# A linear-attention stack: the first half group in front, its causal mask by a product and ScalarE, carried sums by ScalarE, fp4 weights later, spreads from sixteen rows

## Chip, cores and metric

One NeuronCore of a Trainium2 chip. The metric is the device time of one launch in microseconds (us). A TensorE matmul is called a product of TensorE; VectorE is DVE, ScalarE is ACT, GpSimd is POOL and SyncE is SP in the profile.

## The reference

Input x is 8 sequences of 1024 rows of 256 numbers, all float32. Four residual blocks follow each other, each fed with a layer norm of x:

```python
x = x + L0_attn(_layernorm(x))   # linear "flow" attention, 16 heads of 16, with its own FFN (gelu)
x = x + L0_ffn(_layernorm(x))    # 256 -> 1024 relu -> 256
x = x + L1_attn(_layernorm(x))   # softmax attention over 1024 rows, one head of 256
x = x + L1_ffn(_layernorm(x))    # fp4-quantised gate/up (704) and down
```

The linear attention is causal. With q and k the sigmoids of projections, it needs running sums over the rows (cumsum) of k and q, from which per row and head the flows `sink_in` and `src_out` come; then running sums of k and q weighted by these flows; from them a weight for each source row and a scale for each target row; and last the causal product of q with the running sum of k times v:

```python
sink_in = normal / einsum(q + EPS, cumsum(k) + EPS)
src_out = normal / einsum(k + EPS, cumsum(q) + EPS)
cons_sink = einsum(q + EPS, cumsum(k * src_out) + EPS) / normal
cons_src  = clip(einsum(k + EPS, cumsum(q * sink_in) + EPS) / normal, -1, 1)
src_comp = exp(cons_src) / cumsum(exp(cons_src)) * normal
x = einsum(q * sink_in / normal, cumsum(k x (v * src_comp))) * sigmoid(cons_sink)
```

## The kernel before

**Tiling.** Rows go in chunks of 128; a group p is four chunks (512 rows), so there are 16 groups, two to a sequence. The linear attention of a group is `linear_group` (L863). `front` (L873) normalises and transposes a chunk. `linear_span` (L919) works on a span of chunks: the projections and sigmoids (`k`, `q`, [head dimension on partitions, rows along the free axis]); `running` (L806), which is a scan of VectorE along the rows (`prod`); a fused product with the other of q and k (EPS added); `head_sums` (L748), small products with `hsum` that add the 16 dimensions of each head; the reciprocal `r1` and `flow`; the spreading of `flow` from one row per head back to 16 rows; the same with weighted q and k (`weighted`); and from these `e`, `div` and `scale`, and again a spreading, by which q is multiplied. Each of these waits for the one before. Sums that run over a span's end are carried by a copy of the scan's last column (`carry_cur`, `carry_w`). Group 0 alone is cut into two spans of two chunks ("near"); its spreading is done by TensorE with mask tiles (`spread_near`, L785). All other groups spread through memory (`spread`, L763): `flow` is written to a flat DRAM tile, and each of the tiles is read from there with each head's row repeated 16 times.

**Chunks.** `linear_chunk` (L1079) makes v, `qz` (q masked to the even or odd heads by two ScalarE operations), the scores in four PSUM banks of 128x512, their causal mask (`sc`, a product with an upper triangle), the values, the carried sum `kv`, the output product with Wo, a layer norm (`u`, `h`), and the transposes that feed the FFN's half tiles.

**Filling.** `dense` (L1269) is the two FFNs of a group, in halves of 256 rows, 8 steps of 4 products each (`half,w_ff`, then `w_ff,hidden`); a step reads 256 KB of weights through five buffers `w_ff`, whose loads are `load_weights` (L1314). `norms_1`, `norms_2`, `soft_chunk` (softmax attention and the fp4 FFN for a chunk), `fp4_weights` (L645; 18 pieces quantised on VectorE, loaded as `w_raw`, worked with `q_c`) and `softmax_weights` are further parts.

**Order.** All parts are generators. `Plan` (L63) records every instruction in the order in which it takes parts, and this order is pinned on each engine: an engine never passes a waiting instruction. `Plan.took` (L157) holds estimated costs of each operation, a ring time for DMA among them, and `Plan.run` (L267) takes the part that can start first by these estimates, then the riper, then the one with the lower due time `at`. All DMAs are issued by SP, in that order.

Of the kernel before, what the change touches and what calls it, by code (L numbers as in the profile page):

```python
# [9 lines left out]
F32 = mybir.dt.float32  # L10
# [52 lines left out]
class Plan:  # L63
# [12 lines left out]
    def __init__(self, tc, nc):  # L76
# [15 lines left out]
        self.tiled = False  # L92
        self.parts = []
# [63 lines left out]
    def took(self, queue, op, args, kw):  # L157
# [12 lines left out]
        if queue == "tensor":  # L170
# [5 lines left out]
            if tiled:  # L176
                cost *= 0.25
# [24 lines left out]
        for ap in aps:  # L202
            name = ap.tensor.name
            if self.by.get(name) != queue:
                start = max(start, self.done.get(name, 0.0))
            if name not in self.done and name in self.held:
                start = max(start, self.used[name])
        end = start + cost
        if queue == "sync":
            n = 4e-6 / 160e-3  # L210
# [56 lines left out]
    def run(self):  # L267
        while self.parts:
            now = self.free.get("tensor", 0.0)
            best = None  # L270
            for part in self.parts:
# [5 lines left out]
                wait = max(max(t) - now - (0.3 if stays else 0.0), 0.0)  # L277
                unripe = max(t[1] + self.RIPE[queue] - now, 0.0)
# [48 lines left out]
def block_stack_kernel(ctx: ExitStack, tc: tile.TileContext, a: dict, out: bass.AP):  # L327
# [115 lines left out]
    pos = const.tile([P, P], F32, name="pos")  # L443
    nc.vector.tensor_copy(pos, pos_i)
# [20 lines left out]
    mask_tiles = [make("prob", "mask") for _ in range(2)]  # L465
    late = set()

    def masks():
        yield act(ident, at=0.02)
        for b in range(4):  # L470
# [12 lines left out]
    def late_constants():  # L483
# [10 lines left out]
        late.add("hsum")  # L494
        yield dve()
# [3 lines left out]
        for g in range(NG):  # L499
            yield dve()  # L500
            nc.vector.tensor_scalar(rpos[:, g, :], pos, float(g * GT), None, ALU.add)
            yield dve()
            nc.vector.reciprocal(rpos[:, g, :], rpos[:, g, :])
# [141 lines left out]
    def fp4_weights():  # L645
# [15 lines left out]
        for i, (src, turns) in enumerate(pieces):  # L661
            for j in range(i, min(i + 3, len(pieces))):
                if j not in raws:
# [3 lines left out]
                        dma(at=0.9 + 2.2 * i / len(pieces), when=lambda: count["stage"] == 4),  # L667
# [7 lines left out]
            at = 0.9 + 2.2 * i / len(pieces)  # L675
# [87 lines left out]
    def spread(packed, tiles):  # L763


        width = packed.shape[0] // 32 * P
        flat = hbm.tile([32, GT], F32, tag="packed", name="packed", bufs=4)
        yield dma(packed)
        nc.sync.dma_start(
            out=flat[:, :width].rearrange("r (t l) -> t r l", l=P), in_=packed  # L770
        )
        out = {}
        for b in tiles:
            t = out[b] = yield from fresh("flow", dma(flat), "spread")
            nc.sync.dma_start(
                out=t[:, :width],
                in_=bass.AP(
                    tensor=flat.tensor,
                    offset=flat.offset + 8 * b * GT,
                    ap=[[GT, 8], [0, DH], [1, width]],  # L780
# [25 lines left out]
    def running(out, cur, carry, b, first, last):  # L806
# [9 lines left out]
        if not last:  # L816
            nc.vector.tensor_copy(carry[:, b : b + 1], out[:, cur.shape[1] - 1 :])
# [45 lines left out]
    def linear_group(p):  # L863
# [34 lines left out]
        for i in range(G):  # L898
            plan.start(front(i), p + 0.03 * i)
# [19 lines left out]
    def linear_span(p, span, fronts, tiles):  # L919
# [13 lines left out]
        after = 0.25 if span.start else 0.0  # L933
        near = len(span) < G

# [32 lines left out]
        for n, b in enumerate((2, 0, 3, 1)):  # L968
            other = (b + 2) % 4
            prods[other] = yield from fresh(  # L970
                "flow", dve(cur[b], at=p + 0.15 + 0.04 * n + after, when=turn("flow")), "prod"
            )
            prod = prods[other][:, :width]
            running(prod, cur[b], past["cur"], b, opens, closes)
            yield dve(cur[other])
            nc.vector.scalar_tensor_tensor(prod, cur[other], ATT_EPS, prod, ALU.add, ALU.mult)
# [6 lines left out]
        nc.vector.scalar_tensor_tensor(flow, pos[rows], float(g * GT), r1, ALU.add, ALU.mult)  # L983
# [7 lines left out]
        for n, b in enumerate((2, 0, 3, 1)):  # L991
            other = (b + 2) % 4
            w = weighted[b]
            need = dve(w, at=p + 0.35 + 0.04 * n + after, when=turn("scale"))
            if near:
                weighted[b] = yield from fresh("flow", need, "weighted")
            else:
                yield need
            out = weighted[b][:, :width]
            nc.vector.tensor_tensor(out, cur[b], w[:, :width], ALU.mult)  # L1000
            if near and n % 2:
# [620 lines left out]
```

## Time and profile before

| | |
|---|---|
| median of three runs | 2690.91 us (2689.86 to 2692.45) |
| the profiled execution | 2683.94 us |
| its span | 2682.2 us |
| mean granted TensorE clock | 0.991 |
| ACT_TABLE_LOAD | 308, 395.2 us |
| DMA | 209.92 MB, mean 78 GB/s |
| `w_ff` loads | 1024 issues of 128 KB |
| `spread` reads | 90 issues of 256 KB |
| `packed` writes | 30 issues of 64 KB |

A row of instructions gives engine, operation, output and input tile; all of the kernel's own have one line, that of the recorder (L308), so tiles tell them apart. An f32 matmul is recorded as two instructions. In a table of stretches each engine has its busy time and count, then follow the granted TensorE clock (1.00 is full), the share of the 16 DMA engines' time and GB/s.

### The profile page before, as it was taken

The numbers are of one execution on the slowest core, as the hardware profiler recorded it, in microseconds if no ns is written. First come the engines' busy times: TensorE is split into PE (matmuls) and PEld (weight loads), VectorE is DVE, ScalarE is ACT, GpSimd is POOL, SyncE is SP. The second block draws the span as 40 slices with busy tenths as digits, with TensorE's granted clock in tenths as the row PEclk, the third lists the DMA queues.
The fourth block names the chain that finished last, engine by engine and source line by source line (L and its number), as shares of the span: only waits on it lengthen the run. The fifth ranks groups of instructions, "written<-read, shape, count | busy, mean of one in ns | idle before, by whom it ended". The sixth has DMA issues, their size and how long they took to land.

```text
span 2682.2 us, 45602 instructions
## 1 busy us (share of the span) xinstructions
PE 2597.4 (97%) x16687; PEld 2014.0 (75%) x16687; DVE 1969.3 (73%) x4514; ACT 1246.7 (46%) x2430; POOL 560.5 (21%) x1101
## 2 busy tenths in 40 slices
PE   6999999999999999999999999999999999999997
PEld 4777777777777777777777777777777777787765
DVE  8889687776858668686776858778586776856576
ACT  2443445535455453645536354363635536344343
POOL 1232232221212213122131212212121131212000
PEclk8999999999999999999999999999999999999999
DMA  3334222312223222232322223132231322322100
GB/s 87 107 105 143 89 82 64 108 59 89 73 69 106 66 86 73 69 96 71 91 73 76 80 75 106 52 92 75 70 108 54 98 63 71 89 66 81 41 12 12
DMA packets 282135, 209.92 MB, mean 78 GB/s; under 512 B 23864, under 2 KB 270392, under 8 KB 281912
## 3 DMA queue, kind: packets, MB, share of 16 engines
q1 hardware_dynamic: 281912, 207.00, 25.9%
q8 instruction: 133, 2.18, 0.3%
q14 instruction: 90, 0.74, 0.1%
HBM read 188.17 MB, written 18.74 MB: 77 GB/s over the span
## 4 chain that ended last, share of the span: by engine, by line
PE 80%; DVE 12%; DMA 2%; issue 1%; ACT 1%; POOL 1%; SPq 0%; DVEq 0%; ACTq 0%
PE bank L308 80%; DVE hid L308 2%; DVE prod L308 1%; DVE n L308 1%; DVE ln_st L308 1%; DMA spread<-packed 1%; DVE x_amax L308 1%; DVE u L308 1%; DMA w_ff<-in_L_attn_W_dram 1%; DVE res L308 1%; POOL ln_rstd L308 1%; DVE div L308 1%; DVE e L308 0%; DVE q L308 0%; DVE ln_mv L308 0%
## 5 line engine op out<-in xcount | busy, mean ns | idle before, releaser
L308 PE MATMUL bank<-half,w_ff 128*128 128x256 f32 x2048 | 533.6, 383 | 14.5 <-DMA w_ff<-in_L_ffn_w_dram 6.0
L308 PE MATMUL bank<-w_ff,hidden 128*128 128x256 f32 x2048 | 530.4, 383 | 7.7 <-issue 6.6
L308 PEld LDWEIGHTS bank<-half,w_ff 128*128 128x128 f32 x2048 | 379.4, 191 | 91.4 <-issue 26.6
L308 PEld LDWEIGHTS bank<-w_ff,hidden 128*128 128x128 f32 x2048 | 371.1, 191 | 96.0 <-issue 50.7
L308 ACT ACT_TABLE_LOAD x308 | 395.2, 1283 | 75.2 <-PE bank L308 71.1
L308 POOL TENSOR_SCALAR ln_ve<-ln_mv 128x1 f32<-128x1 f32 x384 | 96.0, 250 | 1320.7 <-DVE ln_mv L308 1299.4
L308 ACT ACTIVATE hidden<-bank,c_L_ffn_b 128x256 f32<-128x256 f32 x256 | 121.1, 473 | 338.0 <-PE bank L308 336.7
L308 PE MATMUL bank<-n2T,qT 128*128 128x512 f32 x512 | 241.4, 594 | 0.9 <-ACT qT L308 0.9
L308 POOL TENSOR_TENSOR ln_rstd<-ln_ve,neghalf 128x1 f32<-128x1 f32 x384 | 229.4, 597 | 32.0
L308 PE MATMUL bank<-vt,probT 128*128 128x256 f32 x1024 | 232.2, 380 | 0.0
L308 PEld LDWEIGHTS bank<-vt,probT 128*128 128x128 f32 x1024 | 193.2, 190 | 30.3 <-issue 3.3
L308 ACT ACTIVATE hidden<-bank,c_L_attn_b 128x256 f32<-128x256 f32 x256 | 121.4, 474 | 177.0 <-PE bank L308 175.4
L308 PE MATMUL bank<-wdT,hqT 128*128 128x256 f32 x768 | 178.0, 382 | 1.8 <-ACT hqT L308 1.8
L308 PE MATMUL bank<-wgT,xqT 128*128 128x352 f32 x512 | 173.4, 461 | 1.1 <-ACT xqT L308 0.9
L308 PE MATMUL bank<-wuT,xqT 128*128 128x352 f32 x512 | 172.4, 459 | 0.0
L308 DVE TENSOR_TENSOR sc<-bank,triu 128x512 f32<-128x512 f32 x256 | 159.4, 679 | 5.3 <-PE bank L308 3.8
L308 PEld LDWEIGHTS bank<-wdT,hqT 128*128 128x128 f32 x768 | 145.4, 191 | 22.8 <-ACT hqT L308 2.8
L308 DVE TENSOR_TENSOR hid<-hid,bank 128x352 f32<-128x352 f32 x118 | 60.9, 516 | 133.8 <-PE bank L308 92.0
L308 POOL TENSOR_TENSOR xr<-xr,b_L_attn_ln_b 128x256 f32<-128x256 f32 x64 | 49.3, 788 | 482.6 <-DMA xr<-in_L_attn_inputs_dram 482.6
L308 PEld LDWEIGHTS bank<-n2T,qT 128*128 128x128 f32 x512 | 93.6, 190 | 69.5 <-issue 62.7
L308 PEld LDWEIGHTS bank<-wuT,xqT 128*128 128x128 f32 x512 | 97.3, 190 | 54.2
L308 PEld LDWEIGHTS bank<-wgT,xqT 128*128 128x128 f32 x512 | 92.6, 190 | 37.0 <-issue 3.8
(214 smaller groups left out, 4384.4 us busy)
## 6 DMA issues: line engine op xcount, KB each, us to landing
w_ff<-in_L_attn_W_dram SPq DMA_DIRECT2D x512, 128.0 KB
w_ff<-in_L_ffn_w_dram SPq DMA_DIRECT2D x512, 128.0 KB
spread<-packed SPq DMA_DIRECT2D x90, 256.0 KB
x<-in_L_attn_inputs_dram SPq DMA_DIRECT2D x64, 128.0 KB
xr<-in_L_attn_inputs_dram SPq DMA_DIRECT2D x64, 128.0 KB
rows<-res SPq DMA_DIRECT2D x64, 128.0 KB
out_dram<-y SPq DMA_DIRECT2D x64, 128.0 KB
rows<-rows SPq DMA_DIRECT2D x56, 128.0 KB
```

The lines of the kernel that those rows point to most:

```text
L308: ins = method(*args, **kw)
```

## The change

Seven edits go together.

1. The parts of group 0's first span (chunks 0 and 1) get due times below zero. `Plan.run` calls these urgent: it does not hold them back until they are ripe, and lets them start up to 0.3 us late in front of others.
2. The recorder's estimates: a bf16 product costs a quarter, a product within 2.1 us after 2 us of TensorE's rest costs double, and a DMA's ring time goes by 250 GB/s in place of 160.
3. In group 0 the causal mask is no longer a VectorE product. A bf16 tile `later` (in a `q_c` buffer until group 0's last chunk) holds -2^100 above the diagonal and, in its last 128 columns, the identity; a product of these is put into each score bank first, the scores are added to it, and ScalarE's ReLU copies the bank to `sc`.
4. The carried columns are copied by ScalarE, and scans come in pairs: scan, scan, fused product, fused product.
5. The fp4 weights' due times run from 1.5 to 3.1 in place of 0.9 to 3.1.
6. `spread` writes the flat tile twice, side by side, and reads 16 source rows, each repeated 8 times, in place of 8, each repeated 16 times.
7. `pos` holds the positions of both groups of a sequence, so that `flow`, `e` and `rpos` need fewer operations, and the two products of `kv` with the block diagonal become one.

```diff
@@ Plan.took
-            if tiled:
+            if tiled or op == "matmul" and kw["lhsT"].dtype == BF16:
                 cost *= 0.25
...
+        if queue == "tensor":
+            if start - self.ran > 2.0:
+                self.slow = start + 2.1
+            if start < self.slow:
+                cost *= 2
+            self.ran = start + cost
         end = start + cost
         if queue == "sync":
-            n = 4e-6 / 160e-3
+            n = 4e-6 / 250e-3
@@ Plan.run
-                wait = max(max(t) - now - (0.3 if stays else 0.0), 0.0)
-                unripe = max(t[1] + self.RIPE[queue] - now, 0.0)
+                wait = max(max(t) - now - (0.3 if stays or part[2] < 0.0 else 0.0), 0.0)
+                urgent = part[2] < 0.0
+                unripe = 0.0 if urgent else max(t[1] + self.RIPE[queue] - now, 0.0)
@@ constants
-    pos = const.tile([P, P], F32, name="pos")
-    nc.vector.tensor_copy(pos, pos_i)
+    pos = const.tile([P, NG, P], F32, name="pos")
+    for g in range(NG):
+        nc.vector.tensor_scalar(pos[:, g, :], pos_i, float(g * GT), None, ALU.add)
...
+    later = make("q_c", "later")[:, : GT + P]
...
+        nc.scalar.copy(later[:, GT:], ident)
...
+        nc.vector.tensor_scalar(
+            later[:, :GT].rearrange("p (n t) -> p n t", n=4),
+            triu.unsqueeze(1).to_broadcast([P, 4, P]),
+            -1.0, 2.0**100, ALU.add, ALU.mult,
+        )
@@ fp4_weights
-                        dma(at=0.9 + 2.2 * i / len(pieces), when=lambda: count["stage"] == 4),
+                        dma(at=1.5 + 1.6 * i / len(pieces), when=lambda: count["stage"] == 4),
...
-            at = 0.9 + 2.2 * i / len(pieces)
+            at = 1.5 + 1.6 * i / len(pieces)
@@ spread
-        flat = hbm.tile([32, GT], F32, tag="packed", name="packed", bufs=4)
+        flat = hbm.tile([32, 2, GT], F32, tag="packed", name="packed", bufs=4)
         yield dma(packed)
-        nc.sync.dma_start(
-            out=flat[:, :width].rearrange("r (t l) -> t r l", l=P), in_=packed
-        )
+        for e in range(2):
+            nc.sync.dma_start(out=flat[:, e, :].rearrange("r (t l) -> t r l", l=P), in_=packed)
...
-                    offset=flat.offset + 8 * b * GT,
-                    ap=[[GT, 8], [0, DH], [1, width]],
+                    offset=flat.offset + 8 * b * 2 * GT,
+                    ap=[[GT, 16], [0, DH // 2], [1, GT]],
@@ running
         if not last:
-            nc.vector.tensor_copy(carry[:, b : b + 1], out[:, cur.shape[1] - 1 :])
+            yield act(out)
+            nc.scalar.copy(carry[:, b : b + 1], out[:, cur.shape[1] - 1 :])
@@ linear_group
-            plan.start(front(i), p + 0.03 * i)
+            plan.start(front(i), p + 0.03 * i - (p == 0 and i < 2))
@@ linear_span
-        after = 0.25 if span.start else 0.0
+        after = 0.25 if span.start else -1.0 if near else 0.0
...
-        for n, b in enumerate((2, 0, 3, 1)):
-            other = (b + 2) % 4
-            prods[other] = yield from fresh(
-                "flow", dve(cur[b], at=p + 0.15 + 0.04 * n + after, when=turn("flow")), "prod"
-            )
-            prod = prods[other][:, :width]
-            running(prod, cur[b], past["cur"], b, opens, closes)
-            yield dve(cur[other])
-            nc.vector.scalar_tensor_tensor(prod, cur[other], ATT_EPS, prod, ALU.add, ALU.mult)
+        for n, pair in enumerate(((2, 0), (3, 1))):
+            for b in pair:
+                need = dve(cur[b], at=p + 0.15 + 0.08 * n + after, when=turn("flow"))
+                prod = prods[(b + 2) % 4] = (yield from fresh("flow", need, "prod"))[:, :width]
+                yield from running(prod, cur[b], past["cur"], b, opens, closes)
+            for b in pair:
+                yield dve(cur[b], prods[b])
+                nc.vector.scalar_tensor_tensor(
+                    prods[b], cur[b], ATT_EPS, prods[b], ALU.add, ALU.mult
+                )
...
-        nc.vector.scalar_tensor_tensor(flow, pos[rows], float(g * GT), r1, ALU.add, ALU.mult)
+        nc.vector.tensor_tensor(flow, pos[rows, g, :], r1, ALU.mult)
...
-        nc.vector.scalar_tensor_tensor(e, pos[rows], float(g * GT), e, ALU.add, ALU.mult)
-        nc.vector.tensor_scalar(e, e, src[rows], None, ALU.mult)
+        nc.vector.scalar_tensor_tensor(e, e, src[rows], pos[rows, g, :], ALU.mult, ALU.mult)
@@ linear_chunk
+        at = p - (p == 0 and i < 2)
...
+        by_act = p == 0
...
+        banks = [mm_bank() for _ in range(4)]
+        for bank in banks:
+            if by_act:
+                nc.tensor.matmul(
+                    bank, lhsT=later[:, GT:], rhs=later[:, :GT], start=True, stop=False,
+                    skip_group_check=True,
+                )
...
-                    start=True,
+                    start=not by_act,
...
+            if by_act:
+                nc.scalar.activation(sc, bank.rearrange("p (n t) -> p n t", n=4), AF.Relu)
+                scores.append(sc)
+                continue
...
-            for k in range(2):
-                nc.vector.tensor_tensor(
-                    new[:, k, :].rearrange("p (r d) -> p r d", r=4),
-                    kvbank[:, k, :].unsqueeze(1).to_broadcast([P, 4, 32]),
-                    bdiag.rearrange("p (r d) -> p r d", r=4),
-                    ALU.mult,
-                )
+            nc.vector.tensor_tensor(
+                new.rearrange("p k (r d) -> p k r d", r=4),
+                kvbank.unsqueeze(2).to_broadcast([P, 2, 4, 32]),
+                bdiag.rearrange("p (r d) -> p r d", r=4).unsqueeze(1).to_broadcast([P, 2, 4, 32]),
+                ALU.mult,
+            )
```

## The prediction

> **What bounds the kernel now.** I read the page first (busy shares), then the stretches, then TensorE's waits, then the timeline. The page's first part:
>
> ```profile
> PE 2597.4 (97%) x16687; PEld 2014.0 (75%) x16687; DVE 1969.3 (73%) x4514; ACT 1246.7 (46%) x2430; POOL 560.5 (21%) x1101
> ```
>
> TensorE is the bound: of 2682.2 us only 84.8 are idle. So a change can win in three ways only: less TensorE work, less idle, or less work done at half clock. The stretches say where the idle is (after the stretch and its length: busy time of PE, PEld, DVE, ACT, POOL; clock; DMA share; GB/s):
>
> ```profile
> 0.00:72.30 72.30, 46.75 (x334) 33.78 (x335) 58.35 (x157) 19.40 (x47) 14.27 (x37) 0.80 0.32 81
> 72.30:128.90 56.60, 56.59 (x423) 44.50 (x421) 46.94 (x115) 28.85 (x67) 17.44 (x35) 0.99 0.36 106
> 128.90:150.00 21.10, 14.49 (x91) 11.82 (x91) 20.13 (x38) 5.51 (x16) 8.83 (x12) 0.84 0.57 152
> 200.00:250.00 50.00, 43.90 (x248) 35.53 (x247) 44.64 (x104) 18.93 (x43) 11.92 (x23) 0.93 0.46 138
> 2600.00:2682.20 82.20, 67.76 (x290) 48.55 (x288) 53.77 (x118) 27.49 (x53) 2.95 (x8) 0.97 0.04 13
> ```
>
> 25.6 us idle lie before the first FFN matmul at 72.3, 6.6 in 128.9 to 150, 6.1 in 200 to 250, 14.4 at the end; the 2160 us from 340 to 2500 hold 22.7, 1%. Shorter stretches show the half clock of the front:
>
> ```profile
> 36.00:40.00 4.00, 2.99 (x16) 2.83 (x15) 3.67 (x8) 0.63 (x3) 0.00 (x0) 0.50 0.00 0
> 40.00:44.00 4.00, 4.00 (x15) 2.94 (x15) 2.70 (x8) 0.21 (x1) 0.00 (x0) 0.50 0.00 0
> 44.00:48.00 4.00, 4.00 (x18) 2.89 (x21) 2.81 (x8) 1.70 (x4) 0.00 (x0) 0.50 0.00 0
> 68.00:72.00 4.00, 4.00 (x15) 3.36 (x15) 2.12 (x6) 1.10 (x3) 0.26 (x2) 0.50 0.01 2
> ```
>
> After the idle of 25 to 30 us the clock is 0.50 to about 49, and again from 64 to 73. What TensorE waits for in the first 72.3 us, and later for weights (total us, times, longest):
>
> ```profile
> PE bank L308 <- DVE prod L308: 9.1, 6, 4.3
> PE bank L308 <- DVE scale L308: 3.4, 1, 3.4
> ...
> PE bank L308 <- DMA w_ff<-in_L_ffn_w_dram: 6.0, 2, 5.7
> PE bank L308 <- DMA w_ff<-in_L_attn_W_dram: 5.9, 3, 4.3
> ```
>
> It waits for VectorE's serial chain. Its marks in the timeline (start, length):
>
> ```profile
> 23.10 0.42 DVE L308 TENSOR_TENSOR weighted<-k,bank 128x256 f32<-128x256 f32 x1 [1.73 <-PE bank L308]
> 35.30 0.28 DVE L308 TENSOR_TENSOR e<-bank,rpos 64x128 f32<-64x128 f32 x1
> 40.08 0.28 DVE L308 TENSOR_TENSOR scale<-e,div 64x128 f32<-64x128 f32 x1
> 50.19 4.87 DVE L308 TENSOR_TENSOR sc<-bank,triu 128x512 f32<-128x512 f32 x8
> 65.44 0.29 DVE L308 TENSOR_TENSOR scale<-e,div 64x128 f32<-64x128 f32 x1
> 72.34 1.63 PE L308 MATMUL bank<-half,w_ff 128*128 128x256 f32 x4
> ```
>
> **The front, first span put first.** In the old order VectorE interleaves span 0 (chunks 0, 1) with span 1 (chunks 2, 3); in the new one span 1's scans stand behind. I add old durations in the new order. The first normalised tile goes ahead of the hsum copies and two rpos additions, but a mask operand of 128x512 (0.55, from 0.31 for 128x256) comes in: the first hsum matmuls end at about 19.6 (was 20.05). One group of projections instead of two stands before the first spreading matmuls (1.0 less): `weighted` at 22.0. From there to `e`: 4 products 0.42, 4 scans 0.70, 4 fused products 0.43, two span-1 scans 0.74, waits for ScalarE 0.5: 8.2, so `e` at about 30 (was 35.3). To `scale`: 0.3 + 0.34 + ScalarE 0.6 + matmul and copy 0.6, with two products and a scan of span 1 queued ahead of `div`, then 0.48 + 0.28 + 0.94 + 0.3 + 0.34 + 0.28 (one operation of 0.28 less): about 35 (was 40.1). Transpose, spreading (2.07 at half clock), two q products: q is scaled at 38.2, ScalarE's qz is out at 39.9 (was 46 to 47.8). TensorE is later than that: v projections, 4.1 at half clock, end at 41.6.
>
> **The mask.** Per chunk of group 0: four bf16 matmuls of 128x512 before the scores, then four ReLU copies on ScalarE for four VectorE products of 0.68. No bf16 matmul is in the trace. The nearest row is one recorded instruction of 512 f32 columns (n2T,qT: x4 in 1.88, 0.43 apart); an f32 matmul takes two of them (0.86), the upper end; the lower end is 0.11, a 128-column transpose. I take 0.43, doubled at half clock. Chunk 0's masks end at 45.0. "TensorE: Matmul & The Clock Gate", section "Wait — 56ns, not 53.3ns?", gives 215.7 ns for 512 columns when warm; by it all sixteen would cost 3.5, and the sum would be some 5 us lower. ReLU: the nearest row is ACT prob 128x512, 0.68, the same as VectorE's. From 37.4 to 72.3 ScalarE is busy 6.0 of 34.9 us, VectorE 27.2, so the work goes to the idler engine: 16 x 0.68 = 10.9 us leave it. Queued behind the eight ReLUs on ScalarE are the copies of k and xo (0.37 each), which TensorE awaits.
>
> From 45.0: scores 1.2 to 2, eight ReLUs to 51 to 52, value matmuls, kv by POOL 0.79, second chunk's xo, wo, then u 0.42, statistics 0.6, POOL 0.75, 0.47, h 0.77: chunk 1's h at about 62.5, the first FFN matmul at 63.4 (was 72.3): **-8.9**. Not done by then and done before: one hsum 0.46, total 0.3, transpose 0.2, two v projections 1.72, spreading 1.03: **+3.7**. The first FFN pair ran at half clock before (1.63 against 0.86): **-0.8**. Masks of chunks 2 and 3: 8 x 0.43 = **+3.4**. Span 1's `scale` is now later: VectorE has about 11 us queued ahead of it from 60.7 and ScalarE has Exp between two table loads (1.28 each), so near 75.6 where it was 65.4. What covers it is the first half's FFN, 8 x 1.72 = 13.8, and the wqk products, 4; what sticks out I put at **+2**, from 0 to 5.
>
> The clock page (same title, "What's actually happening") has the array warm after about 3.4 us of sustained work. The rows differ: 40 to 48 are fully busy and still at 0.50. By the page the new front would be warm from 39 and some 3 us shorter; I go by the rows.
>
> **Carried sums by ScalarE.** 72 VectorE copies of 0.15 (0.25 to 0.3 with the gaps before and after) become ScalarE copies of 0.15. New wait: the fused product overwrites the sum that ScalarE reads, so VectorE stands until the copy is through; behind it are the other products of its queue and, for TensorE, the hsum matmuls. Scans go in pairs, so one wait per pair, 0.3, up to 1.3 behind a table load: 4 pairs in each of 8 opening groups, from -0.5 to +1.3 each. Past 340 us VectorE is 73% busy and TensorE 99%: **0**. Without that cover it would be up to 42. The merged kv product (112 x 0.28 to 56 at about 0.48), the merged e and flow: VectorE alone, **0**.
>
> **Fp4 weights later, spreads.** The 18 pieces keep their DMAs and about 3 us of VectorE each; they only leave 73 to 150, where VectorE is at 83 to 95%. TensorE's waits for n and w_raw from 140 to 340 are 3.4; fewer pieces ahead of n on VectorE take about half: **-1.5** (0 to -3.4). Each spread's flat copy is written twice: 30 more SP issues of 0.57, 64 KB each, ahead of weight loads on SP; SP's issues are not what ends TensorE's waits, so 0 to +1 in each group, taken 0. The reads of 256 KB (x90) take 16 source rows in place of 8. The 5.7 wait at 129 comes with four such reads in flight:
>
> ```profile
> 128.90:135.00 6.10, 0.38 (x3) 0.20 (x3) 5.89 (x10) 0.33 (x2) 0.65 (x1) 0.72 0.92 224
> ```
>
> Share 0.92 at 224 GB/s: nearly all engines already work, so 1 MB takes some 4.7 us whatever its split. "DMA: Bandwidth & Descriptors", section "Why a DMA increments its semaphore by 16 and not by 1", holds that a DMA goes over as many engines as divide its outermost dimension, so 8 before. By it the four reads shrink by about 4 us and the two long waits nearly go, some 10 off; the share speaks for less. The two waits (5.7, 4.3) and their half-clock restarts (1.3, 1.5) are 12.8: from 0 to -12.8, and as weights still queue behind the spread I take half: **-6.4**.
>
> **Sum.** The end (14.4 idle) is the last chunk's chain, which no edit touches; a new order may move it by some us either way: 0. -8.9 + 3.7 - 0.8 + 3.4 + 2 - 1.5 - 6.4 = -8.5. The profiled execution took 2683.94 (span 2682.2, 1.7 around it), so 2675.4; the median of the runs, 2690.91, is 7.0 above it, so 2682.4.
>
> **Rivals.** *A, both gains in full.* FFN starts near 58 (mask matmuls at the low end, no waits in span 1) and both weight waits go: -13 + 3.7 + 1 - 13 = -21, 2670. For it: 25.6 idle in front. Against: the chain of VectorE stays serial.
> *B, given back.* FFN starts earlier, but span 1, now behind, leaves TensorE without work at the second half, and weights are as late as before: -8.5 + 6.4 + 3 = about +1, 2692. For it: VectorE was 81% busy in the front.
> *C, slower.* The recorder takes the rings at 250 GB/s instead of 160, and so orders FFN matmuls ahead of weights that have not landed. Pure FFN takes 256 KB in 1.72 us (152 GB/s) beside the spreads, and the trace's best in 4 us is 244. Its place is the weight wait in each of the 15 later groups; at 1.3 us each, 20 - 8.5 = +11, 2702. It decides from (8.5 + 5.4) / 15 = 0.93 each. Against: after 340 those waits were 1.9 in total.
>
> **Numbers.** A measurement of this kernel tells 0.2%, 5.4 us, from no change. Forecast (2676 to 2688) 0.42, A 0.22, B 0.22, C 0.14. Faster takes A and nine tenths of the forecast (the rest is above 2685.5), 0.6; same gets B's larger part, 0.23; slower C and what is left of B, 0.17. The range 2666 to 2698 leaves out A's far end and most of C.
>
> **What would show it.** Right: the first FFN matmul near 63; `e` and `scale` of span 0 near 30 and 35; no `sc` by VectorE before 150; the wait for w_ff in 125 to 150 under 3 us; idle from 340 on within 5 us of before. Wrong: a long wait of TensorE for span 1's `scale` or ScalarE's `sc` after 63, or w_ff waits in every group.

## The result: a little slower, and the profile after

The changed kernel takes 2694.57 us (median of 12 runs, 2686.36 to 2699.39), the kernel before, run beside it, 2691.81 (12 runs, 2685.18 to 2696.22): a ratio of 1.0012, 95% interval [1.0003, 1.002]. The forecast was 2682.4 and "faster". The profiled execution after took 2695.86 us (span 2694.2), 1.3 above its median; the one of before lies about 8 below its own, so the two profiles differ by 12 us where the medians differ by 2.8. Of a difference between the two profiles some 9 us are such chance.

The page's first part, after:

```profile
PE 2607.3 (97%) x16701; PEld 2021.4 (75%) x16703; DVE 1942.7 (72%) x4353; ACT 1261.6 (47%) x2521; POOL 587.6 (22%) x1101
```

VectorE is relieved as the change says (1969.3 to 1942.7 us), ScalarE takes some of it, TensorE has 9.9 us more busy time, and its idle time (span less busy) is 86.9, from 84.8.

The stretches of the front and of the weight waits, after (stretch, length, busy time of PE, PEld, DVE, ACT, POOL, clock, DMA share, GB/s):

```profile
0.00:72.30 72.30, 50.45 (x356) 37.19 (x358) 48.01 (x129) 30.56 (x77) 15.04 (x39) 0.81 0.30 84
72.30:128.90 56.60, 52.90 (x400) 39.89 (x400) 45.80 (x113) 27.87 (x73) 17.34 (x32) 0.97 0.32 93
128.90:150.00 21.10, 17.25 (x101) 13.97 (x100) 18.90 (x38) 5.99 (x14) 6.48 (x11) 0.92 0.63 172
200.00:250.00 50.00, 44.11 (x245) 34.40 (x243) 38.45 (x82) 19.79 (x51) 11.34 (x21) 0.97 0.47 137
```

Up to 72.3 TensorE is busy 3.7 us longer than before, from 72.3 to 128.9 it is busy 3.7 us less, from 128.9 to 150 2.8 more. The front's gain in busy time is given back in the next stretch, and 2.7 us of the 3.7 lie near 100: TensorE waits 1.84 for `n` and 0.85 for `h`.

The marks of the front in the timeline, after (start, length):

```profile
27.97 0.42 DVE L316 SCALAR_TENSOR_TENSOR prod<-k,prod 128x256 f32<-128x256 f32 x1 [2.11 <-ACT carry_w L316]
...
34.62 0.28 DVE L316 TENSOR_TENSOR e<-bank,rpos 64x128 f32<-64x128 f32 x1 [0.93 <-PE bank L316]
...
38.86 0.28 DVE L316 TENSOR_TENSOR scale<-e,div 64x128 f32<-64x128 f32 x1
...
76.54 0.29 DVE L316 TENSOR_TENSOR scale<-e,div 64x128 f32<-64x128 f32 x1
```

```profile
62.97 1.59 PE L316 MATMUL bank<-half,w_ff 128*128 128x256 f32 x4 [0.46 <-ACT half L316]
```

The first FFN product starts at 62.97 (before 72.34, forecast 63.4); span 0's `e` and `scale` are at 34.62 and 38.86 (before 35.30 and 40.08), not at 30 and 35. The first line shows one reason: VectorE waits 2.11 us for ScalarE's copy of one column (`carry_w`, at 27.75), which is queued behind a ScalarE operation that itself waits for TensorE. The other is the clock. The stretches of 14 to 28 us, after and then before:

```profile
14.00:18.00 4.00, 1.46 (x10) 0.55 (x8) 2.84 (x7) 1.59 (x8) 2.32 (x3) 1.00 0.16 41
20.00:24.00 4.00, 4.00 (x15) 3.16 (x15) 1.23 (x3) 0.47 (x1) 0.00 (x0) 0.50 0.85 236
24.00:28.00 4.00, 4.00 (x14) 3.24 (x13) 1.82 (x5) 0.75 (x3) 0.00 (x0) 0.50 0.53 130
```

```profile
14.00:18.00 4.00, 2.46 (x15) 1.47 (x13) 3.65 (x10) 1.68 (x5) 1.27 (x2) 1.00 0.65 191
20.00:24.00 4.00, 4.00 (x27) 3.39 (x26) 2.10 (x4) 0.95 (x2) 0.00 (x0) 1.00 0.60 158
24.00:28.00 4.00, 1.43 (x8) 0.74 (x8) 3.69 (x11) 1.96 (x3) 0.00 (x0) 1.00 0.88 133
```

TensorE rests more from 14 to 18 (1.46 busy in place of 2.46), and the clock drops to 0.50 from 19.1 on; before it dropped only at 29.2. That the rest brings the drop is a reading of these rows. TensorE then does span 1's projections and the spreading (3.78 us for what took 2.05) at half clock, fully busy and slow.

The waits for weights (total, times, longest), after:

```profile
PE bank L316 <- DMA w_ff<-in_L_attn_W_dram: 5.0, 2, 4.4
...
PE bank L316 <- DMA w_ff<-in_L_ffn_w_dram: 0.7, 2, 0.6
```

5.7 us, from 11.9: that fall is near the forecast. The wait of 5.7 at 129 has become 3.29 for `w_raw` and 0.72 for `w_ff`; the one at 230 has stayed (4.44, from 4.28).

### The profile page after: what moved, and what is told of

The parts are those of the page before. It is cut to its first block, busy times and chain, and to the rows that moved or that the text cites. A ratio compares the mean times of both kernels' runs of the same rounds, so it can differ in the third digit from the quotient of the medians.

```text
span 2694.2 us, 45562 instructions
## 1 busy us (share of the span) xinstructions
PE 2607.3 (97%) x16701; PEld 2021.4 (75%) x16703; DVE 1942.7 (72%) x4353; ACT 1261.6 (47%) x2521; POOL 587.6 (22%) x1101
## 4 chain that ended last, share of the span: by engine, by line
PE 76%; DVE 16%; DMA 3%; ACT 2%; issue 2%; POOL 1%; SPq 1%; DVEq 0%; ACTq 0%
PE bank L316 76%; DVE prod L316 3%; DVE hid L316 2%; DMA spread<-packed 2%; DVE n L316 1%; DVE ln_st L316 1%; DVE spread L316 1%; DVE u L316 1%; ACT L316 1%; DVE res L316 1%; DVE x_amax L316 1%; DVE mx L316 1%; DVE ln_mv L316 1%; SPq L316 1%; DVE div L316 0%
## 5 line engine op out<-in xcount | busy, mean ns | idle before, releaser
L316 PE MATMUL bank<-w_ff,hidden 128*128 128x256 f32 x2048 | 536.4, 385 | 0.0
L316 DVE TENSOR_TENSOR sc<-bank,triu 128x512 f32<-128x512 f32 x240 | 149.4, 681 | 19.7 <-PE bank L316 18.2
L316 DVE TENSOR_REDUCE mx<-bank 128x1 f32<-128x512 f32 x128 | 86.9, 679 | 59.7 <-PE bank L316 59.6
```

What stands on the lines that cost most here:

```text
L316: ins = method(*args, **kw)
```

## The experiments

Each kernel was timed beside the kernel before. What an edit costs when undone is read against the changed kernel's 1.0012. An interval covers the executions of one kernel, not the choice of its order, and every edit here makes the recorder find a new order for all the engines.

### One edit undone at a time

**The carried columns copied by VectorE again.**

```diff
-            yield act(out)
-            nc.scalar.copy(carry[:, b : b + 1], out[:, cur.shape[1] - 1 :])
+            nc.vector.tensor_copy(carry[:, b : b + 1], out[:, cur.shape[1] - 1 :])
+            yield dve()
```

> The changed kernel, with the carried columns copied by VectorE again (scans still in pairs). The first theory, that the change lost its gain in ScalarE's queue: in the changed kernel VectorE stood 34.3 us (28.0 + 6.3, longest 4.1) for these copies, and ScalarE stood 41.8 us for the scans. It expects those rows gone, span 0's e at 31 to 32 us (34.6 in the changed kernel, 35.3 before), the first FFN matmul before 61, and 4 to 8 us less than the changed kernel: ratio to before 0.9985 or lower. Its rival, that these waits lie beside TensorE's work: within 2 us of the changed kernel (ratio 1.0005 to 1.002).

Measured 2698.49, ratio 1.0039 [1.0028, 1.0051]. VectorE's waits for these copies are real in the changed kernel:

```profile
DVE prod L316 <- ACT carry_cur L316: 28.0, 15, 4.1
...
DVE prod L316 <- ACT carry_w L316: 6.3, 12, 2.1
```

34.3 us in all, some 1.3 for each wait where the prediction took 0.3 per pair, and yet undoing the edit costs time. VectorE has 28% to spare from 340 to 2500; that the waits are covered by it is the reading. The copies do delay the front: without them `e` is at 32.86 and the first FFN product at 61.14, both 1.8 earlier than in the changed kernel, and the kernel is still slower. Neither expectation foresaw a loss.

**The mask by VectorE's product again.** The bf16 product of group 0 goes, with the two operations that fill `later`, and `by_act` is false everywhere, so that `sc` is the product with `triu` in group 0 too.

```diff
-    later = make("q_c", "later")[:, : GT + P]
...
-        nc.scalar.copy(later[:, GT:], ident)
...
-        nc.vector.tensor_scalar(
-            later[:, :GT].rearrange("p (n t) -> p n t", n=4),
...
-        by_act = p == 0
+        by_act = False
...
-        for bank in banks:
-            if by_act:
-                nc.tensor.matmul(
-                    bank, lhsT=later[:, GT:], rhs=later[:, :GT], start=True, stop=False,
-                    skip_group_check=True,
-                )
```

> The changed kernel, with group 0's causal mask as VectorE's product again (no mask matmuls, no ReLU). The theory that the mask matmuls cost TensorE more than the front wins by them (16 products, 1.04 us for four in the changed kernel's timeline, so 4.1 us) expects 3 to 5 us less than the changed kernel: ratio 0.9995 to 1.0005. The rival, that VectorE's relief (10.9 us) is what brings the FFN forward: the first FFN matmul 4 to 6 us later than 63, and 1 to 3 us more than the changed kernel.

Measured 2700.96, ratio 1.0046 [1.0029, 1.0062]: with its order the edit gains, and its matmuls are cheap (of the 16, 14 are in the trace, 4.6 us in all, half clock included). The rival expectation had the time go the right way, by too little, but not its reason: without the edit the first FFN product comes 8.4 us earlier than in the changed kernel, not later.

```profile
30.45 0.28 DVE L316 TENSOR_TENSOR e<-bank,rpos 64x128 f32<-64x128 f32 x1 [1.12 <-PE bank L316]
34.63 0.28 DVE L316 TENSOR_TENSOR scale<-e,div 64x128 f32<-64x128 f32 x1
54.55 1.13 PE L316 MATMUL bank<-half,w_ff 128*128 128x256 f32 x4 [0.46 <-ACT half L316]
```

```profile
14.00:18.00 4.00, 2.44 (x14) 1.24 (x12) 3.29 (x7) 1.95 (x8) 1.15 (x2) 1.00 0.60 164
20.00:24.00 4.00, 3.69 (x24) 3.25 (x24) 2.50 (x6) 1.04 (x4) 0.00 (x0) 1.00 0.67 191
0.00:129.00 129.00, 98.47 (x749) 74.56 (x750) 96.42 (x234) 52.12 (x127) 33.02 (x73) 0.93 0.32 90
```

The urgent parts are the same here, but TensorE rests less from 14 to 18 and the clock drops at 29.2 only, as it did before; `e` and `scale` then stand at the 30 and 35 of the forecast. Whether the operations that fill `later` or only the new order bring the early drop, no run separates. And yet this is one of the slower kernels: up to 129 its TensorE has 749 recorded matmul instructions and is idle for 30.5 us, against 755 and 25.5 in the changed kernel. An earlier start of the FFN did not make it faster.

**The fp4 weights' due times from 0.9 again.**

```diff
-                        dma(at=1.5 + 1.6 * i / len(pieces), when=lambda: count["stage"] == 4),
+                        dma(at=0.9 + 2.2 * i / len(pieces), when=lambda: count["stage"] == 4),
...
-            at = 1.5 + 1.6 * i / len(pieces)
+            at = 0.9 + 2.2 * i / len(pieces)
```

> The changed kernel, with the fp4 weights' due times from 0.9 again. The theory that the later due times cost (in the changed kernel TensorE stood 3.3 us for one piece at 130 and 2.7 us for a scale at 150, with pieces queued ahead on VectorE; the pieces still run then) expects 2 to 5 us less than the changed kernel: ratio 0.9995 to 1.0005. The rival, that they relieve VectorE while it is the busiest: 3 to 8 us more, ratio 1.002 to 1.004.

Measured 2699.16, ratio 1.0036 [1.0022, 1.005]: it gains too.

**No due times below zero.** `front`, `linear_span` and `linear_chunk` of group 0's chunks 0 and 1 get their old times, and `Plan.run` knows no urgent parts.

```diff
-            plan.start(front(i), p + 0.03 * i - (p == 0 and i < 2))
+            plan.start(front(i), p + 0.03 * i)
...
-        after = 0.25 if span.start else -1.0 if near else 0.0
+        after = 0.25 if span.start else 0.0
...
-        at = p - (p == 0 and i < 2)
+        at = p
```

> The changed kernel without due times below zero: span 0 and span 1 interleaved again on VectorE, all else as changed. The theory that putting span 0 first brings nothing net, since span 1's scale then comes at 76.5 (65.4 before) and TensorE stands 2.7 us for its products at 98 to 101, expects the first FFN matmul at 66 to 70 (63.0), span 1's scale before 70, and a time within 2 us of the changed kernel. The rival, that the front's gain (first FFN matmul 72.3 to 63.0) is real: 3 to 6 us more, ratio 1.0025 to 1.0035.

Measured 2690.34, ratio 1.0003 [0.9992, 1.0014]: the first half group put in front, which begins the FFN 7.4 us earlier (62.97, from 70.40 in this run), is worth nothing that can be measured beside the other edits.

**The spread of 8 rows and one flat copy.**

```diff
-        flat = hbm.tile([32, 2, GT], F32, tag="packed", name="packed", bufs=4)
+        flat = hbm.tile([32, GT], F32, tag="packed", name="packed", bufs=4)
...
-        for e in range(2):
-            nc.sync.dma_start(out=flat[:, e, :].rearrange("r (t l) -> t r l", l=P), in_=packed)
+        nc.sync.dma_start(out=flat.rearrange("r (t l) -> t r l", l=P), in_=packed)
...
-                    offset=flat.offset + 8 * b * 2 * GT,
-                    ap=[[GT, 16], [0, DH // 2], [1, GT]],
+                    offset=flat.offset + 8 * b * GT,
+                    ap=[[GT, 8], [0, DH], [1, GT]],
```

> The changed kernel, with each spread reading 8 source rows again and the flat tile written once. The theory that a spread is bounded by the DMA engines' time and not by its split expects no loss: VectorE's waits for spread data no longer than in the changed kernel (31.0 us over 21), the w_ff wait at 225 to 235 still 4 to 5 us, the time within 2 us of the changed kernel (ratio 1.000 to 1.002). The rival, that 8 rows use half the engines: VectorE's waits for spread data grow by 10 us or more, w_ff waits by 3 to 6 us, and the kernel is 4 to 8 us slower than the changed one (ratio 1.003 to 1.004).

Measured 2706.14, ratio 1.0066 [1.0047, 1.0085]. TensorE's waits for weights go from 5.7 us to 17.7:

```profile
PE bank L316 <- DMA w_ff<-in_L_ffn_w_dram: 9.4, 5, 6.3
PE bank L316 <- DMA w_ff<-in_L_attn_W_dram: 8.3, 3, 3.0
```

The rival also had VectorE's waits for the spreads grow by 10 us or more; they fell, to 26.4 us from 31.0 in the changed kernel.

**The ring estimate at 160 GB/s.**

```diff
-            n = 4e-6 / 250e-3
+            n = 4e-6 / 160e-3
```

> The changed kernel, with the recorder's ring time by 160 GB/s again; the work is the same, the order differs. The kernel before with 250 GB/s waited 29.0 us for w_ff where it had waited 11.9, and was 1.0056 of before. The theory that the ring time is the part of the change that loses, and the sixteen-row spread only pays it back, expects w_ff waits of 0 to 4 us (5.7 in the changed kernel) and 5 to 12 us less than the changed kernel: ratio 0.997 to 0.9995. The rival, that 250 fits the sixteen-row spread (its reads are faster), and that a time too long only brings products of other parts forward: 1.001 to 1.004.

Measured 2681.37, ratio 0.9971 [0.996, 0.9982]: one constant of the recorder's estimates, which adds or removes no instruction, decides between faster and slower. Of six edits undone, this is the only one whose removal clearly gains: 0.41%, 11 us.

### One edit done alone in the kernel before

**The ring estimate at 250.**

```diff
-            n = 4e-6 / 160e-3
+            n = 4e-6 / 250e-3
```

> The kernel before, with one number of the recorder changed: a DMA's ring time by 250 GB/s in place of 160. No instruction is added or taken away, only the order differs. The theory that a new order by itself moves this kernel little expects 0.999 to 1.001. The rival, that the optimistic ring time puts products ahead of weights which have not landed, expects TensorE's waits for w_ff to rise from 11.9 us to 18 or more and a ratio of 1.002 or more.

Measured 2704.95, ratio 1.0056 [1.0039, 1.0073]. The waits for weights of TensorE, 11.9 us before, are now:

```profile
PE bank L308 <- DMA w_ff<-in_L_ffn_w_dram: 20.6, 11, 6.3
PE bank L308 <- DMA w_ff<-in_L_attn_W_dram: 8.4, 4, 5.2
```

29.0 us: products ordered ahead of weights that have not landed, which is rival C's mechanism, in 15 waits.

**The spread of 16 rows.** The edit of `spread` in the change (point 6), with nothing else; of its lines, the read:

```diff
-                    ap=[[GT, 8], [0, DH], [1, width]],
+                    ap=[[GT, 16], [0, DH // 2], [1, GT]],
```

> The kernel before, with the spread alone changed (two flat copies, 16 source rows); the recorder counts one DMA more in each spread. The theory that sixteen rows put the reads on twice as many engines expects w_ff waits of 0 to 4 us (11.9 before), VectorE's waits for spread data of 10 us or less (21.2 before), and 4 to 9 us less than before: ratio 0.9965 to 0.9985. The rival, that the order alone made the difference between the changed kernel and the one with eight rows: 0.9995 to 1.002, w_ff waits of 8 us or more.

Measured 2697.53, ratio 1.0028 [1.0019, 1.0038]. TensorE waits less for weights, but the time doesn't follow, which neither expectation had:

```profile
PE bank L308 <- DVE v L308: 11.9, 12, 1.7
PE bank L308 <- DMA w_ff<-in_L_ffn_w_dram: 4.1, 3, 2.8
PE bank L308 <- DMA w_ff<-in_L_attn_W_dram: 0.2, 1, 0.2
```

The weight waits are 4.3 us, from 11.9, and those for VectorE's `v` 11.9, from 2.5. VectorE's own waits for the spreads are 23.3 us, from 21.2: for it the sixteen rows brought nothing.

### The ring estimate at other values: rule or chance

A single re-recorded order could be a poor draw. So the estimate was varied alone, in the changed kernel and in the one before (the diff is that one constant each time).

> The changed kernel with the ring estimate at 150 GB/s: all work is the same, only the order that the recorder finds differs. Estimate theory (an estimate that is too fast puts work ahead of what it waits for, one near or below the true rate does not): near the version with 160 (0.997 of before), 2676 to 2687, and TensorE's waits for w_ff under 8 us. Chance theory (every re-recorded order of this kernel falls anywhere within some 0.5 per cent, and 160 was a good draw): anywhere from 2675 to 2705, with no relation to 160.

> The changed kernel with the ring estimate at 200 GB/s. Estimate theory: between the version with 160 (0.997 of before) and the changed kernel (1.001), 0.997 to 1.002 of before. Chance theory: anywhere from 0.994 to 1.006, outside that stretch in about half the cases.

> The changed kernel with the ring estimate at 225 GB/s. Estimate theory (the loss begins where the estimate passes what the rings give): between the version with 200 (0.9974) and the changed kernel (1.0012). Chance theory (250 was a poor draw of the order, draws scatter by 0.15 per cent about 0.998): 0.996 to 1.000.

> The changed kernel with the ring estimate at 300 GB/s. Estimate theory: no better than with 250, 1.001 to 1.005 of before, and the waits of TensorE for w_ff above the 5.7 us of the changed kernel. Chance theory: 0.996 to 1.000, with no growth of those waits.

> The kernel before with the ring estimate at 150 GB/s in place of 160, and nothing else. Estimate theory: within 0.2 per cent of before, 2683 to 2694, w_ff waits of TensorE about the 11.9 us of before. Chance theory: before's own order was the pick of many, so another one costs some 0.2 to 0.6 per cent, 2694 to 2705, as 250 GB/s did (1.0056).

> The kernel before with the ring estimate at 200 GB/s. Estimate theory: between before and its version with 250 GB/s (1.0056), 1.000 to 1.005, and w_ff waits between 11.9 and 29.0 us. Chance theory: w_ff waits without relation to the estimate, the time anywhere from 0.998 to 1.008.

| estimate, GB/s | changed kernel: ratio to before | kernel before: ratio | quotient |
|---|---|---|---|
| 150 | 0.9985 [0.9975, 0.9995] | 1.0023 [1.0014, 1.0032] | 0.9962 |
| 160 | 0.9971 [0.996, 0.9982] | 1 | 0.9971 |
| 200 | 0.9974 [0.9963, 0.9985] | 1.0015 [1.0005, 1.0025] | 0.9959 |
| 225 | 1.0003 [0.999, 1.0015] | | |
| 250 | 1.0012 [1.0003, 1.002] | 1.0056 [1.0039, 1.0073] | 0.9956 |
| 300 | 1.0031 [1.0022, 1.0041] | | |

Two things stand in this table. From 160 up the changed kernel gets slower with every step of the estimate, 0.6% in all (the steps from 160 to 200 and from 225 to 250 lie within the intervals); the kernel before does so too. That speaks for the estimate and against an order that falls anywhere. But chance has its share: 150 is worse than 160 in both, and the kernel before with 150 came out where the theory of chance had it. And the rest of the change gains at each of the four estimates that were run with and without them: 0.29 to 0.44%, on the mean 0.38%, 10 us.

In the kernel before the loss goes with the waits for weights: 11.9, 19.3 and 29.0 us with 160, 200 and 250. In the changed kernel it isn't the weights: beside 250 its TensorE doesn't wait for `w_ff` once between 1000 and 2500 us, and in the version with 300 the weight waits are 5.5 us in the whole run, against the 5.7 that the expectation wanted exceeded. It is idle time in the long even stretch. The stretch 1000 to 2500, with 250 and then with 160:

```profile
1000.00:2500.00 1500.00, 1478.89 (x9485) 1152.73 (x9484) 1077.34 (x2390) 724.70 (x1403) 332.96 (x617) 1.00 0.27 80
```

```profile
1000.00:2500.00 1500.00, 1490.32 (x9554) 1164.00 (x9553) 1071.36 (x2403) 714.80 (x1399) 336.67 (x617) 1.00 0.27 80
```

21.1 us idle against 9.7, which is most of the 14.5 us between the two profiled spans (11 between the medians). In the same stretch the changed kernel's waits of TensorE (the two longest) and VectorE's waits for DMA:

```profile
PE bank L316 <- DVE n L316: 5.6, 3, 2.2
PE bank L316 <- DVE v L316: 4.8, 5, 1.1
```

```profile
DVE spread L316 <- DMA spread<-packed: 10.4, 5, 2.6
DVE q L316 <- DMA spread<-packed: 7.1, 7, 1.9
```

With 160 VectorE waits there for DMA in two places alone:

```profile
DVE spread L316 <- DMA spread<-packed: 6.4, 2, 3.6
```

The reading is that by 250 GB/s a spread is due sooner than it lands, the order puts VectorE's product with it earlier, and VectorE stands at it with `v` and `n` queued behind. The timeline bears it out in part: three times (near 1030, 1676 and 2324) TensorE waits first for `n` and then for `v`, 8.9 us in all, 6 to 8 us after VectorE's waits for a spread (near 1022, 1668 and 2316); with 160 there is no such pair. Most of the other 12 us follow no such wait. Across the versions the reading does not hold: with 300 VectorE waits 27.7 us for spreads and TensorE is idle for 24.5, but with 225 it is 5.7 and 20.2, and with 200 18.4 and only 13.7. So how the estimate costs time in the changed kernel is argued, not shown. Idle time of TensorE from 1000 to 2500 over the versions: 12.5 and 12.9 us with 150; 4.1 to 20.7 with 160 (six kernels); 13.7 to 22.9 with 200 (three); 20.2 with 225; 17.9 to 23.0 with 250 (seven); 24.5 with 300.

### The two gains of the forecast beside an estimate of 160

Each of these kernels is the changed one with the diff of the estimate (160, once 200) and those of the urgent parts, of the spread, or of both, shown above.

> The changed kernel with the ring estimate at 160 GB/s and without due times below zero for the first half group. The first FFN product then falls back from 63 to 70 or later. If the front's term holds (-8.9 + 3.7 + 2, some 3 to 5 us won), this is 0.1 to 0.2 per cent slower than the version with 160 alone: 0.998 to 0.999 of before. If the gain of the front is all given back (rival B), it is the same as that version, 0.997, or better.

> The changed kernel with the ring estimate at 160 GB/s and the spread of 8 source rows and one flat copy. If the weights' term holds (-6.4), TensorE's waits for w_ff are some 10 to 18 us and the time is 0.2 to 0.3 per cent above the version with 160 alone: 0.999 to 1.001 of before. If the sixteen rows only matter beside an estimate of 250 GB/s, it is within 0.1 per cent of that version, 0.996 to 0.998.

> The changed kernel with the ring estimate at 160 GB/s, no due times below zero and the spread of 8 rows: what is left of the change is the mask, the carried columns, the fp4 weights' times, the merged operations and the two clock estimates. If the two edits each cost 0.3 per cent by themselves: 0.990 to 0.993 of before. If the two single orders were lucky: 0.994 to 0.998.

> The same with the ring estimate at 200 GB/s, where the version with both edits has 0.9974. If the two edits cost time by themselves: 0.991 to 0.994. If the single orders at 160 were lucky: 0.995 to 0.999. Weights: the wait of TensorE for w_ff at 125 to 150 us comes back to 4 us or more, since the reads of 8 rows are back.

| ratio to before, estimate 160 | 16 rows | 8 rows |
|---|---|---|
| first half group urgent | 0.9971 [0.996, 0.9982] | 0.9943 [0.9928, 0.9958] |
| not urgent | 0.9941 [0.9928, 0.9953] | 0.9919 [0.9905, 0.9932] |

Beside 160 the urgent front costs 0.24 and 0.30%, the sixteen rows 0.22 and 0.28% (and 0.28% alone in the kernel before): both of the forecast's gains are losses there. Without them the kernel takes 2666.76 us, 22.4 less than the kernel before beside it. The version with 8 rows and urgent parts missed both of its expectations too: its waits for `w_ff` are 6.4 us, not 10 to 18. At 200, though, the version without both edits has 1.0013 [1.0002, 1.0025], while with both it had 0.9974: outside both expectations, and the other way round. It reads as if the sixteen rows let the order stand a faster estimate: from 160 to 200 the version without both goes from 0.9919 to 1.0013, and from 160 to 250 the urgent one with 8 rows from 0.9943 to 1.0066, while with 16 rows 160, 200 and 250 give 0.9971, 0.9974 and 1.0012. But a step of 0.94% where the kernel before moves by 0.15% also says how much one order can differ from the next. The expected long weight wait is there in the version at 200: 5.42 us, just before 123.

Why the urgent front doesn't pay shows in the stretches 0 to 129 and 129 to 340, both with 160 and 16 rows, urgent first:

```profile
0.00:129.00 129.00, 104.42 (x758) 77.87 (x760) 94.60 (x244) 58.91 (x150) 32.01 (x71) 0.88 0.34 89
129.00:340.00 211.00, 194.70 (x1482) 153.55 (x1483) 160.29 (x364) 85.36 (x197) 57.20 (x107) 0.96 0.39 114
```

```profile
0.00:129.00 129.00, 101.49 (x753) 75.08 (x754) 90.20 (x216) 61.08 (x141) 31.38 (x71) 0.91 0.36 95
129.00:340.00 211.00, 198.78 (x1519) 156.25 (x1518) 173.70 (x423) 90.91 (x220) 61.59 (x119) 0.98 0.40 114
```

Urgent, TensorE is busy 2.9 us longer up to 129, but at a lower clock (five more instructions in it), and from 129 to 340 4.1 us less, with 37 fewer. The reading is that the products which fill the waits of the urgent front are missing when span 1 and the fp4 weights come; which products, no run shows. The version without both, the best of all, has its gain mostly in the long even stretch, and none in the front: 4.1 us idle from 1000 to 2500, where the kernel before has 16.8, and 30.3 up to 129, from 25.6.

```profile
1000.00:2500.00 1500.00, 1495.90 (x9599) 1172.48 (x9598) 1082.68 (x2421) 725.26 (x1413) 337.61 (x623) 1.00 0.26 79
```

## Why the prediction was wrong, point by point

The account is a way through the versions at 160, each a step from one measured kernel to the next, so its sum is the measured ratio by construction: before to the version without both edits −0.81% (−21.8 us: mask, carried columns, fp4 times, merged operations, the estimates of the clock and of bf16); the urgent front on top +0.24% (+6.5); the sixteen rows +0.28% (+7.5); the estimate of 250 +0.41% (+11.0): +3.2 us, the ratio of 1.0012. By another order of steps the parts differ.

- **The step that failed: the ring estimate, left out of the sum.** The working costed edit 2 at nothing and kept it as rival C, at 0.14, in the form of weight waits in every group, with "after 340 those waits were 1.9 in total" against it. That row holds for an order made with 160; it can't speak for one made with 250. Measured: +0.41% in the changed kernel (11 us), +0.56% in the kernel before (15 us, with 17.1 us more waits for weights). C's 20 us for 15 groups were too many. In the kernel before it came as C had it; in the changed kernel not by the weights, and the way is open (8.9 us of it stand behind VectorE's waits for spreads).
- **What would show it.** Four of the signs named came true (first FFN product near 63, no `sc` by VectorE before 150, `w_ff` waits in 125 to 150 under 3 us, idle from 340 on within 5: 44.0 us, from 41.2), only `e` and `scale` did not, and still the kernel was not faster. The sign of idle time past 340 was drawn too wide: with 160 it is 35.2.
- **The sum without it.** With 160 the kernel is 7.4 us faster than before, and the rest of the change gains 10 us on the mean over four estimates; the forecast was −8.5. That agreement is luck, owed to errors that cancel: the front and the weights, forecast at −4 and −6.4, cost 6.5 and 7.5 in the way above, and what was forecast at +3.4, 0 and −1.5 came with −21.8.
- **The front.** The first FFN product at 62.97 (63.4 forecast) is right by luck. `e` came 4.6 late and `scale` 3.9; the masks of chunk 0, cheaper than taken, ended at 46.6 (45.0 forecast), and from there to the FFN it took 16.4 in place of 18.4. The −8.9 as a gain is not right: with what the same working gave back (+3.7, −0.8, +2) it came to −4, and measured beside 160 the edit costs 6.5 to 8. That is rival B's outcome; its mechanism is seen only in the 2.7 us near 100. `e` came late for two reasons: VectorE's waits for the carry copies (2.11 and 0.80 after `weighted`, where 0.5 was taken, and 0.90 and 0.26 before it), and a half clock from 19.1 on, since the durations were old ones, measured at full clock. In the run without the copies it is 1.8 earlier, in the one without the early drop of the clock 4.2. Where the clock stayed full to 29.2, without the mask's edit, the marks stand where the working put them (30.45 and 34.63). The working counted what TensorE would be spared and not what a rest between goes with in its clock. The first FFN pair ran mostly at half clock all the same (1.59 for −0.8 foreseen), and span 1's `scale` came at 76.54 (75.6 foreseen).
- **The mask.** +3.4 was taken for TensorE and nothing, outside the front, for VectorE's 10.9 us. Four of its matmuls in a row, in chunk 2, took 1.03 us from the first start to the last end, about 0.26 each where 0.43 was taken, so some 2.1 of the 3.4, and undoing the edit costs 0.34% (9 us): a gain, mis-sized in sign. It is not the gain that the working meant, an earlier FFN: with this edit the first FFN product comes 8.4 later. No wait of TensorE for `sc` followed.
- **Carried sums: 0 forecast.** The waits were 34.3 us, and undoing the edit costs 0.27%. The cover named (VectorE at 73%) fits that; in the front the copies cost 1.8.
- **Fp4 times: −1.5 forecast**, undone +0.24% (6 us). The waits for `n` and `w_raw` from 140 to 340 fell from 3.4 to 1.4, but one of 3.29 for `w_raw` came at 133. For these three undone edits it is open how much belongs to the edit and how much to the order that came with it; their sum of 0.85% is near the 0.81% of the version that has them without the two others, but with 200 that version gains nothing (1.0013, with 1.0015 for the kernel before).
- **Weights and spreads.** The waits fell about as the −6.4 had it: 11.9 to 5.7 in the whole change, 11.9 to 4.3 with sixteen rows alone. The Trainium skill, "DMA: Bandwidth & Descriptors", section "Why a DMA increments its semaphore by 16 and not by 1", has the outermost dimension set the number of engines; the working's estimate from it was that both long waits nearly go, some 10 us. One went, the other stayed at 4.44. But a wait that goes is not time that goes: sixteen rows alone cost 0.28%, with TensorE's waits for `v` up by 9.4 us. Beside 250 they gain 0.54%.
- **The clock.** The Trainium skill, "TensorE: Matmul & The Clock Gate", section "What's actually happening", has the array warm after about 3.4 us of sustained work; the rows of after again differ, 20 to 28 us being fully busy at 0.50. Going by the rows was right, and not carried far enough.

## What to carry to other kernels

Where a recorder or scheduler fixes the order by estimates, a changed estimate is an edit of its own, and can outweigh the edits that it comes with: vary it alone, over several values and in the kernel before too, ahead of judging the rest. Don't book an earlier start as a gain until you can say what fills TensorE in the stretch after it, and at what clock (the first FFN product came at 54.55, 62.97 and 70.17 in kernels of 1.0046, 1.0012 and 0.9919); and don't book a wait that goes until you know which wait comes second. Of a kernel whose order is re-recorded, a single comparison of a few tenths of a per cent speaks of the order as much as of the edit.

## What the runs showed that was not expected

- TensorE's half clock can outlast full work: the changed kernel has 10.2 us at 0.50 from 19.1 on, of which 20 to 28 are fully busy. And late in the run a short rest is followed by a short drop: a wait of 3.63 us for `prob`, up to 339.47, by 4 us at a mean of 0.58; near 1678 and 2326 there is a drop after two waits close together, 1.80 and 1.09, and 2.21 and 1.09. The kernel before had no drop between 245 and 2650.

```profile
336.00:340.00 4.00, 0.53 (x5) 0.53 (x6) 3.86 (x11) 1.36 (x4) 1.99 (x4) 1.00 0.17 56
340.00:344.00 4.00, 4.00 (x13) 3.23 (x12) 3.75 (x11) 2.72 (x6) 1.95 (x5) 0.58 0.22 61
344.00:348.00 4.00, 4.00 (x16) 2.76 (x16) 3.79 (x10) 1.00 (x3) 2.18 (x5) 1.00 0.23 70
```

- With nothing but the order changed, the changed kernel moved from 0.9971 to 1.0031 of before, two to three times the width of a single comparison's interval, while TensorE's share of busy time stayed at 97%.
